# Reading split weights and first operand pairs into the place of their low parts, in a Perceiver block kernel

## The chip, the core and the metric

The kernel runs on one core of a Trainium2 chip. The metric is the device time of one execution in microseconds (us). TensorE (PE) multiplies matrices, VectorE (DVE), ScalarE (ACT) and GpSimd (POOL) work on elements, and SyncE (SP) issues most DMAs. Each engine works through its own instructions in order, and semaphores tie the engines together.

## What is computed

For 2048 tokens (32 sequences of 64) of width 512 the reference adds three residual parts to `x`, each behind a layer norm: a cross attention over a context of 256 rows per sequence, a latent attention with 16 heads, and a feed-forward part. What matters here are the last two:

```python
out = einsum('bshc,hdc->bshd', softmax(scores) @ kv, wkv_b[:, NOPE:])
x = x + out.reshape(bs, seq_len, H * VD) @ wo_w.T + wo_b      # "wo"
h = square(relu(layernorm(x) @ up_w))                         # "up"
y = h @ down_w + (x @ expert_weight) * sum_of_top2(logits)    # "down"
x = x + layernorm(y) * gamma + beta
```

All arithmetic is float32. The kernel gets that precision from fp32r matmuls: every operand is split into a high part (the value rounded to fp32r) and a low part (value minus high part), and a product is three matmuls (high·high, low·high, high·low).

## The kernel before, in words

The program is one function, `perceiver_block`, under a tile framework. The framework lays tiles out in pools of on-chip memory (a pool with `bufs=n` has n rooms that turn), places the semaphore waits, and orders each engine's instructions by the order of the code and by when its own planning takes them to be ready; `with after(x)` (line 135) keeps an instruction behind x on x's engine. The stages, in order:

1. **Cross attention and query/key preparation** (lines 165 to 585).
2. **Latent attention** (lines 587 to 892): 32 units j of (4 head groups g) x (8 token blocks blk). A unit's values are summed on POOL (`b_w`, line 798) and stored to DRAM tiles `v_d` (`store_v`, line 809). In the same loop every big weight is prepared for later: `prep_w` and `prep_sums` (lines 614, 631) write it to a DRAM tile `w_d[what, k]`.
3. **wo** (loop from line 1003): the output projection, as a seven-product scheme of 2x2 blocks. The work is 64 units u = (token block, slot k); k runs over `ORDER = (0, 1, 5, 6, 7, 2, 3, 4)`, and a unit is 21 matmuls (`seven`, line 692) of one operand pair with one weight slot. The first 16 units mix blocks 0 and 1, so that the slots are needed one by one. Layer norm, turned activations and the small expert product of each block are woven in (`o_sum`, `o_norm`, `o_t`, `o_expert`, lines 920 to 998).
4. **up** (from line 1109): 4 token blocks b of 512 x 8 slots n, 42 matmuls each (`up_seven`), followed by a combine on DVE and a squared ReLU on ACT; the results go to DRAM tiles `h_d` (`store_h`, line 1147).
5. **down** (loop from line 1303): again 64 units of `seven`, with pairs read from `h_d`.

Two kinds of operand are read from DRAM and split before PE can use them.

- A **weight slot** is 128 x 7 x 256 float32, 0.918 MB. `read_slot` (line 638) reads it into a room of the pool `cwp` (2 rooms of 8 KB per partition, tiles `cw_...`). `put_slot` (line 643) then fills the slot's own tiles `wh_...` (tag h) and `wl_...` (tag l) by `split` (line 138) in two slices: ACT casts `c` to `h`, DVE computes `l = c - h`. A slot k has one pair of tiles, used in turn by wo, up and down. The pools of slots 0 and 1 exist from the start of latent attention; those of 4, 3, 2, 7, 6, 5 are laid out after it (line 894) over memory that attention's tiles held.
- An **operand pair** (128 x 7 x 128, 0.459 MB) is read by `read_pair` (line 666) into a small room (`c...`, `oc...`) and split by `left` (line 683) into one of three rotating tiles `hl`.

The places that the change touches, as they stand before:

- slots 0 and 1 for wo are read at g = 3, blk = 3 (line 827) and put at blk = 5 and 6; slot `ORDER[2]` is read behind the loop (line 862), `ORDER[3]` at line 880, each later one just ahead of a `put_slot` in the unit loop at `SLOT_AT = (3, 5, 7, 9, 11)`;
- pairs 0 and 1 are read into halves of a `cwp` room (lines 847 to 850);
- the first four up slots are read and put in units 56, 58, 60, 62 of wo (line 1032); four more at the start of up;
- block 7's sums `oo7` use the single room `o` of the pool `ap` (line 917) that block 6's sums leave when their store to `x2_d` has landed;
- in the last block of up (b = 3) slot `ORDER[n+1]` for down is read into `cwp` at step n, and slot `ORDER[n]` is put behind step n, n = 0 to 4; the last three are put in units 1, 3, 5 of down.

Of the kernel before, what the change touches and what calls it, by code (L numbers as in the profile page):

```python
# [9 lines left out]
FP = mybir.dt.float32  # L10
FR = mybir.dt.float32r
# [7 lines left out]
P = 128  # L19
# [32 lines left out]

SLOT_AT = (3, 5, 7, 9, 11)
EXPERT_AT = (15, 16, 17, 18)
TURN_AT = (19, 22, 28, 34, 42, 50, 58)
MULT_AT = (21, 25, 31, 39, 47, 55, 63)

BETA_AT = 60
# [21 lines left out]
def perceiver_block(ctx: ExitStack, tc: tile.TileContext, x, mem, mask, wq_a, bq_a, qnw, wq_b, bq_b,  # L80
# [3 lines left out]
    def pool(name, bufs=1, **kw):  # L84
        return tc.tile_pool(name=name, bufs=bufs, reuse_waits="tile", **kw)
# [92 lines left out]
    with ExitStack() as mla:  # L178
# [409 lines left out]
        with ExitStack() as pb:  # L588
# [4 lines left out]
            one = pb.enter_context(pool("b_one"))  # L593
            sp = pb.enter_context(pool("b_s", 4))
            pp = pb.enter_context(pool("b_p", 2))
            vp = pb.enter_context(pool("b_v", 2))
            qp = pq.enter_context(pool("b_q", 6))
            gap(pq.enter_context(pool("gap10")), 128, "qh1")
            wqs[1] = pq.enter_context(pool("b_w1", 2))
# [34 lines left out]

            def load_slot(k, what):
                put_slot(k, what, read_slot(k, what))

            def read_slot(k, what, cp=None):
                c = (cp or cwp).tile([P, 8, TB], FP, tag="cw", name=f"cw_{what}{k}")[:, 0:7]
                nc.sync.dma_start(c, w_d[what, k])  # L640
                return c

            def put_slot(k, what, c, engine=nc.vector, pins=(None, None)):

                h = slots[k].tile([P, 7, TB], FR, tag="h", name=f"wh_{what}{k}")
                l = slots[k].tile([P, 7, TB], FR, tag="l", name=f"wl_{what}{k}")
                for a in (slice(0, 4), slice(4, 7)):
                    split(h[:, a], l[:, a], c[:, a], engine, pins)
                wts[k] = (h, l)
# [6 lines left out]

            wts = {}

# [7 lines left out]
            def read_pair(u, src, room=None):  # L666
# [14 lines left out]
                cps[u] = c  # L681

            def left(u, room=None, pins=(None, None)):

                hl = room or hlp.tile(0, name=f"hl{u}")
                hl = hl.rearrange("p a n -> p (a n)")
                h, l = (hl[:, 7 * P * i : 7 * P * (i + 1)].rearrange("p (a n) -> p a n", a=7) for i in range(2))
                low = split(h, l, cps.pop(u), pins=pins)
                ops[u] = (h, l)
                return low  # L690
# [123 lines left out]
            gap(ctx.enter_context(pool("gap1", side="right")), 64, "hl")  # L814
            hls = [ctx.enter_context(pool("hl0", side="right"))]
            hlp = Turns(hls)
# [5 lines left out]
            for j in range(n):  # L822
                g, blk = units[j]
                if blk == 0 and g < 3:
                    load_q(2 * g + 2)
                    load_q(2 * g + 3)
                if g == 3 and blk == 3:
                    cs_wo = [read_slot(k, "wo") for k in range(2)]
                t = []

                def between(behind):
                    if j >= 1:
                        b_d(units[j - 1], ss[j - 1], behind)
                    if j >= 2:
                        t.append(b_t(units[j - 2], ss.pop(j - 2)))
                        return copies[-1]

                qs[j], pins = b_q(units[j], between)
                v = b_v(units[j - 2], *t) if j >= 2 else None
                if v and j < n - 1:  # L840
                    v = b_w(*v)
                if g < 3 and 1 <= blk <= 6:
                    split_q(2 * g + 2 + (blk - 1) // NKQ, (blk - 1) % NKQ, pins)
                if g == 3 and blk in (5, 6):
                    put_slot(blk - 5, "wo", cs_wo.pop(0), pins=pins)
                if j == n - 2:
                    pair_room = cwp.tile([P, 8, TB], FP, tag="cw", name="cw_c").rearrange("p a n -> p (a n)")
                    part = lambda i: pair_room[:, 896 * i : 896 * i + 896].rearrange("p (a n) -> p a n", n=P)
                    for u in range(2):
                        read_pair(u, from_v, lambda: part(u))  # L850
                if j == n - 1:
                    left(0, pins=pins)
                ss[j], sub, most = b_s(units[j], qs.pop(j))
                if loaded:
                    with after(sub):
                        prep_sums(*loaded.pop(0))
                if preps:
                    loaded.append(prep_w(*preps.pop(0)))
                if v and j < n - 1:
                    store_v(*v)  # L860

            cs_wo = [read_slot(ORDER[2], "wo")]
            pq.close()
            ps_p = pc.enter_context(pool("o_psp", space=PSUM))
            for i in range(2):
                hls.append(ctx.enter_context(pool(f"hl{i + 1}", side="right")))
            hlp.pools = hls
            gap(ctx.enter_context(pool("gap2", side="right")), 64, "c")
# [9 lines left out]
            left(2)  # L878
            with after(reads[-1]):
                cs_wo.append(read_slot(ORDER[3], "wo"))  # L880
            read_pair(4, from_v)
# [34 lines left out]
    def o_steps(blk, ps):  # L916
        o = ap.tile([P, 5, TB], FP, tag="o", name=f"oo{blk}")
        return o, combine(ap.tile([P, TB], FP, tag="p1", name=f"op1_{blk}"), ps, o, [])
# [81 lines left out]
    mos = {0: ap.tile([P, 2, D], FP, tag="mo", name="mo0")}  # L1000
    put_slot(ORDER[2], "wo", cs_wo.pop(0))
    xt, xns, xT, x2s, read = {}, {}, {}, {}, 5
    for u, (blk, k) in enumerate(out_units):
# [7 lines left out]
        if u >= 2:  # L1011
# [8 lines left out]
            o, steps = o_steps(blk, pss[blk]) if k == ORDER[-1] else (None, None)  # L1020
            seven(pss[blk], k, *ops.pop(u), steps)
        if u in SLOT_AT:
            i = 3 + SLOT_AT.index(u)
            if i < 7:
                with after(reads[-1]):
                    cs_wo.append(read_slot(ORDER[i + 1], "wo"))
            put_slot(ORDER[i], "wo", cs_wo.pop(0), pins=low)
        if u == 10:
            xt[0] = o_load(0)
        if u in EXPERT_AT:  # L1030
            load_expert(EXPERT_AT.index(u))
        if u - 8 * (NB - 1) in (0, 2, 4, 6):
            load_slot(ORDER[(u % 8) // 2], "up")
        if u in TURN_AT:
# [15 lines left out]
        if u in MULT_AT:  # L1050
# [3 lines left out]
            if i < NB - 2:  # L1054
                next(scaled)
    xr, xc = {}, {}

    def read_x(b, kk, room=None):
# [3 lines left out]
        xc[kk] = (t, None if room else t)  # L1062

    def sum_x(b, kk, behind):

        t, w = xc[kk]
        if w is None:
            w = cwp.tile([P, 8, TB], FP, tag="cw", name=f"xc{b}_{kk}")
            xc[kk] = (t, w)
        with after(behind):  # L1070
            sums([t[:, d] for d in range(4)] + [w[:, d] for d in range(4, 8)], RIGHT)

    def right(b, part, pins=(None, None)):
# [8 lines left out]
        with after(pins[low]):  # L1082
            for sl in [slice(1, 8)] if c is w else [slice(1, 4), slice(4, 8)]:
                to, src = slice(sl.start - 1, sl.stop - 1), (c if sl.start == 1 else w)[:, sl]
                if low:
# [6 lines left out]
    for kk in range(2):  # L1092
        read_x(0, kk)
        sum_x(0, kk, pows[-1])
# [10 lines left out]
    with ExitStack() as pu:  # L1105
# [51 lines left out]
        right(0, 3)  # L1157
        up_c = [read_slot(k, "up") for k in ORDER[4:6]]
        for b in range(NB // 2):
            if b == NB // 2 - 1:  # L1160
                first = [(blk, k) for ks in (ORDER[:5], ORDER[5:]) for blk in DOWN[:2] for k in ks]
                out_units[:] = first + [(blk, k) for blk in DOWN[2:] for k in ORDER]
            if b == NB // 2 - 1:
                cs = [read_slot(ORDER[0], "down")]
            for n, k in enumerate(ORDER):
# [4 lines left out]
                if b == 0 and n in (1, 2):  # L1170
                    read_x(1, n - 1, lambda: ccp.tile([P, 8, P], FP, tag="c", name=f"xp{n}").rearrange(
                        "p (a b) n -> p a (b n)", b=2))
                if b == NB // 2 - 1 and n < 6:
                    cs.append(read_slot(ORDER[n + 1], "down"))
                if b == NB // 2 - 1 and n in (5, 6):
# [16 lines left out]
                if b == 0 and n < 4:  # L1192
                    put_slot(ORDER[n + 4], "up", up_c.pop(0), pins=pins)
                    if n < 2:
                        up_c.append(read_slot(ORDER[n + 6], "up"))
                if b == NB // 2 - 1 and n < 5:
                    put_slot(k, "down", cs.pop(0), pins=pins)
                if b == NB // 2 - 1 and n == 2:
# [21 lines left out]
    with ExitStack() as pd:  # L1220
# [82 lines left out]
        for u, (blk, k) in enumerate(out_units):  # L1303
# [19 lines left out]
            if u in (1, 3, 5):  # L1323
                put_slot(ORDER[5 + u // 2], "down", cs.pop(0))
            if u == 1:
                cs.append(read_slot(ORDER[7], "down"))
            outs = [d for d in outs if step(d, low)]
# [52 lines left out]
```

## Time and profile before

| | |
|---|---|
| median of 3 runs | 1113.07 us (1111.52 to 1113.95) |
| the profiled execution's own time | 1114.92 us |
| its span, from first to last instruction | 1113.1 us |
| PE busy | 1069.7 us, 96% of the span |
| DVE, ACT, POOL busy | 772.9, 547.6, 508.0 us |
| DMA | 254.67 MB, mean 229 GB/s |
| wo stage (first `seven` to first `up`) | about 553 to 784 us |
| up stage | 784 to 943 us |
| down stage | 943 to 1113 us |

The profile is one execution seen by the hardware profiler. Times count from the span's start. In a timeline row the columns are start, duration, engine, line of the code, operation, output tile <- input tiles, shape, count, and in brackets the idle time of that engine just before, with what ended it. In a row by stretches the columns are the stretch and its length, the busy time and count of PE, of PE's weight loads, of DVE, ACT and POOL, then the granted PE clock (1.00 is full), the busy share of the DMA engines and GB/s. Lines that are shared helpers (L141 and L143 are the two halves of every split) are told apart by their tiles.

### The profile page before, as it was taken

Reading aid. Unit: us, or ns where it says so; the run is one execution under the profiler, and the core shown is the slowest. Engines: PE = TensorE matmul, PEld = TensorE weight load, DVE = VectorE, ACT = ScalarE, POOL = GpSimd, SP = SyncE. Lnnn points to the kernel's source line nnn. Section 1 sums busy time; section 2 is a strip of 40 time slices with the busy share of each in tenths; the row PEclk is TensorE's granted clock in tenths of the full one; section 3 lists DMA queues with packets and bytes.
Section 4 is the critical chain, followed back from the end, with each engine's and each line's share of the span. In section 5 each row is a group of like instructions: output and inputs, shape, how many; then the busy total and the mean of one; then the engine's idle time right before and its main releaser. Section 6 shows DMA issues by size and latency. Waiting matters only on the chain.

```text
span 1113.1 us, 25983 instructions
## 1 busy us (share of the span) xinstructions
PE 1069.7 (96%) x10182; PEld 984.6 (88%) x10182; DVE 772.9 (69%) x1363; ACT 547.6 (49%) x1048; POOL 508.0 (46%) x694
## 2 busy tenths in 40 slices
PE   8899999999999999999989999998999998999896
PEld 6677777679999999999889999998999998999896
DVE  4666666647666667666878866668776577688796
ACT  4344444433444434433556544445676667564553
POOL 2333333326778777775471100002058770056761
PEclk9999999999999999999999999998999999999999
DMA  8777666343676787772498776776755789998681
GB/s 260 224 229 231 210 213 209 113 159 126 250 243 236 252 285 265 254 250 105 141 363 298 248 240 227 219 265 232 242 189 193 238 291 279 297 314 254 205 246 59
DMA packets 195386, 254.67 MB, mean 229 GB/s; under 512 B 18544, under 2 KB 140032, under 8 KB 195264
## 3 DMA queue, kind: packets, MB, share of 16 engines
q1 hardware_dynamic: 190848, 241.45, 66.1%
q10 hardware_dynamic: 3456, 8.39, 2.1%
q0 software_dynamic: 960, 3.18, 0.9%
q8 instruction: 80, 1.31, 0.5%
q14 instruction: 42, 0.34, 0.1%
HBM read 146.67 MB, written 106.30 MB: 227 GB/s over the span
## 4 chain that ended last, share of the span: by engine, by line
PE 59%; DMA 12%; DVE 11%; POOL 7%; issue 6%; ACT 4%; SPq 1%; DVEq 0%; POOLq 0%; ACTq 0%
PE up L1115 10%; PE pss L749 6%; PE psq L173 4%; PE psq L174 4%; PE psq L175 4%; PE psv L793 3%; PE op L702 2%; PE op L701 2%; PE op L699 2%; PE psc L367 2%; DMA cw_down<-wd_down 2%; DVE hl L143 2%; PE pse L173 2%; PE pse L175 2%; PE pse L174 2%
## 5 line engine op out<-in xcount | busy, mean ns | idle before, releaser
L731 DVE SCALAR_TENSOR_TENSOR qe<-pse,bqp,cq 64x256 f32<-64x256 f32 x256 | 123.8, 483 | 79.4 <-PE pse L175 73.3
L1115 PE MATMUL up<-xr,wh_up 128*128 128x256 f32 x896 | 154.8, 278 | 2.9 <-ACT up L154 2.9
L1115 PEld LDWEIGHTS up<-xr,wh_up 128*128 128x128 f32 x896 | 136.6, 190 | 3.1 <-ACT up L154 3.1
L701 PE MATMUL op<-wh_wo,hl 128*128 128x256 f32 x448 | 125.5, 280 | 4.8 <-DVE hl L143 4.7
L701 PE MATMUL dp<-wh_down,hl 128*128 128x256 f32 x448 | 124.9, 279 | 4.4 <-DVE hl L143 4.4
L143 DVE TENSOR_TENSOR hl<-c,hl 128x896 fp32r<-128x896 f32 x85 | 96.8, 1140 | 45.5 <-ACT hl L141 45.4
L699 PE MATMUL dp<-wh_down,hl 128*128 128x256 f32 x448 | 124.4, 278 | 1.5 <-DVE uo L159 1.5
L699 PE MATMUL op<-wh_wo,hl 128*128 128x256 f32 x448 | 125.5, 280 | 0.3 <-ACT hl L141 0.3
L702 PE MATMUL op<-wl_wo,hl 128*128 128x256 f32 x448 | 124.4, 278 | 0.1
L702 PE MATMUL dp<-wl_down,hl 128*128 128x256 f32 x448 | 124.4, 278 | 0.0
L1115 PE MATMUL up<-xr,wl_up 128*128 128x256 f32 x448 | 122.9, 278 | 0.0
L141 ACT CAST hl<-c 128x896 fp32r<-128x896 f32 x85 | 79.9, 943 | 76.0 <-PE op L702 33.2
L173 PE MATMUL psq<-qa_hi,qh 128*128 128x256 f32 x384 | 112.7, 294 | 0.0
L174 PE MATMUL psq<-qa_hi,ql 128*128 128x256 f32 x384 | 106.6, 278 | 0.0
L175 PE MATMUL psq<-qa_lo,qh 128*128 128x256 f32 x384 | 106.5, 277 | 0.0
L701 PEld LDWEIGHTS op<-wh_wo,hl 128*128 128x128 f32 x448 | 84.4, 188 | 6.5 <-DVE hl L143 6.4
L701 PEld LDWEIGHTS dp<-wh_down,hl 128*128 128x128 f32 x448 | 84.8, 189 | 5.1 <-DVE hl L143 5.0
L699 PEld LDWEIGHTS dp<-wh_down,hl 128*128 128x128 f32 x448 | 84.8, 189 | 1.7 <-issue 1.7
L699 PEld LDWEIGHTS op<-wh_wo,hl 128*128 128x128 f32 x448 | 84.2, 188 | 1.1 <-issue 0.7
L702 PEld LDWEIGHTS dp<-wl_down,hl 128*128 128x128 f32 x448 | 84.8, 189 | 0.0
L1115 PEld LDWEIGHTS up<-xr,wl_up 128*128 128x128 f32 x448 | 84.8, 189 | 0.0
L702 PEld LDWEIGHTS op<-wl_wo,hl 128*128 128x128 f32 x448 | 84.4, 189 | 0.3 <-DVE wl_wo L143 0.3
(227 smaller groups left out, 3152.8 us busy)
## 6 DMA issues: line engine op xcount, KB each, us to landing
c<-vd SPq DMA_DIRECT2D x58, 448.0 KB, 4.3
cx<-in_ctx SPq DMA_DIRECT2D x32, 512.0 KB, 4.6
vd<-vw SPq DMA_DIRECT2D x29, 512.0 KB, 3.8
hd<-uo SPq DMA_DIRECT2D x107, 128.0 KB, 3.4
hd<-uw SPq DMA_DIRECT2D x21, 512.0 KB, 3.0
dcw<-hd SPq DMA_DIRECT2D x18, 448.0 KB, 5.7
vd<-v SPq DMA_DIRECT2D x30, 256.0 KB, 3.3
c<-hd SPq DMA_DIRECT2D x17, 448.0 KB, 5.8
```

The source lines that it names most:

```text
L141: copy = nc.scalar.copy(hi, src)
L143: return copy, engine.tensor_tensor(lo, src, hi.bitcast(FP), ALU.subtract)
L173: nc.tensor.matmul(ps, ah, bh, start=(j == 0), stop=False)
L174: nc.tensor.matmul(ps, al, bh, start=False, stop=False)
L175: nc.tensor.matmul(ps, ah, bl, start=False, stop=(j == n - 1))
L699: first = nc.tensor.matmul(ps[s // 2][:, s % 2], h[:, a], wh[:, b], start=(k == 0 and s % 2 == 0), stop=False)
L701: nc.tensor.matmul(ps[s // 2][:, s % 2], l[:, a], wh[:, b], start=False, stop=False)
L702: ins = nc.tensor.matmul(ps[s // 2][:, s % 2], h[:, a], wl[:, b], start=False, stop=last)
L731: rope = nc.vector.scalar_tensor_tensor(qe[64 * a : 64 * a + 64, :], pe[r, :], bqp[r, p : p + 1], cq[r, a, :], ALU.add, ALU.mult,)
L749: nc.tensor.matmul(ps[64 * j : 64 * j + 64, pj, b, :], qs[2 * pj + j][a][:, sl], kT[:, a, kt], start=(a == 0), stop=(a == 1),)
L793: nc.tensor.matmul(o, kv[a, i, :], t[a, bp, :], start=True, stop=True)
L1115: nc.tensor.matmul(ps[s // 2][:, s % 2], w[:, i, kk], xr[b, 2 * kk + low][:, j], start=(first and m == 0), stop=(last and m == len(parts) ...
```

## The change

- `read_slot` reads a slot straight into its own `l` tile (`home=True`); `put_slot` casts from there to `h` and subtracts in place. `cwp` is then no longer passed through. With `home=False` the slot waits in a `cwp` room as before: this is kept for `ORDER[2]` and `ORDER[3]` of wo, which are now read during attention (g = 3, blk = 4 and 5).
- Pairs 0 and 1 are read into the second half of their `hl` tile (`read_home`); the pool `hl1` is laid out before attention ends. Room for it comes from `b_s` (4 to 2 buffers) and a gap.
- wo slots `ORDER[4..7]` are read at units 1, 2, 4, 6 and put where they were. Up slots `ORDER[0..3]` are read behind units 57, 58, 59, 61 and put behind 58, 60, 61, 63; `ORDER[4]` is read behind 62.
- `oo7` takes a `cwp` room. The rearranged activations of up's first block are read into `c` rooms, with one `cwp` room for their sums; so their split takes two slices instead of one.
- In up's last block slot `ORDER[n-1]` for down is read at step n (n > 0) and slot `ORDER[n-2]` put behind step n (n = 2 to 6); `ORDER[7]` is read in unit 0 of down.

```diff
-SLOT_AT = (3, 5, 7, 9, 11)
+READ_AT, SLOT_AT = (1, 2, 4, 6), (3, 5, 7, 9, 11)
+UP_READ, UP_PUT = (1, 2, 3, 5, 6), (2, 4, 5, 7)
-            sp = pb.enter_context(pool("b_s", 4))
+            sp = pb.enter_context(pool("b_s", 2))
...
+            def room_of(k, what):
+                return [slots[k].tile([P, 7, TB], FR, tag=a, name=f"w{a}_{what}{k}") for a in ("h", "l")]
+            def read_slot(k, what, home=True, behind=None):
+                hl = room_of(k, what) if home else None
+                c = hl[1].bitcast(FP) if home else cwp.tile([P, 8, TB], FP, tag="cw", name=f"cw_{what}{k}")[:, 0:7]
+                with after(behind):
+                    read_slots[what, k] = hl, c, nc.sync.dma_start(c, w_d[what, k])
+            def put_slot(k, what, pins=(None, None)):
+                hl, c, _ = read_slots.pop((what, k))
+                h, l = hl or room_of(k, what)
                 for a in (slice(0, 4), slice(4, 7)):
-                    split(h[:, a], l[:, a], c[:, a], engine, pins)
+                    split(h[:, a], l[:, a], c[:, a], pins=pins)
...
+            def read_home(u, src):
+                blk, k = out_units[u]
+                homes[u] = hlp.tile(0, name=f"hl{u}")
+                cps[u] = homes[u].rearrange("p a n -> p (a n)")[:, 7 * P :].rearrange("p (a n) -> p a n", a=7).bitcast(FP)
+                reads.append(nc.sync.dma_start(cps[u], src(blk, k)))
...
                 if g == 3 and blk == 3:
-                    cs_wo = [read_slot(k, "wo") for k in range(2)]
+                    for k in range(2):
+                        read_slot(k, "wo")
+                if g == 3 and blk in (4, 5):
+                    read_slot(ORDER[blk - 2], "wo", False)
...
-        o = ap.tile([P, 5, TB], FP, tag="o", name=f"oo{blk}")
+        if blk < NB - 1:
+            o = ap.tile([P, 5, TB], FP, tag="o", name=f"oo{blk}")
+        else:
+            o = cwp.tile([P, 8, TB], FP, tag="cw", name=f"oo{blk}")[:, 0:5]
...
+        if u in READ_AT:
+            read_slot(ORDER[4 + READ_AT.index(u)], "wo", behind=reads[-1])
         if u in SLOT_AT:
-            i = 3 + SLOT_AT.index(u)
-            if i < 7:
-                with after(reads[-1]):
-                    cs_wo.append(read_slot(ORDER[i + 1], "wo"))
-            put_slot(ORDER[i], "wo", cs_wo.pop(0), pins=low)
+            put_slot(ORDER[3 + SLOT_AT.index(u)], "wo", pins=low)
-        if u - 8 * (NB - 1) in (0, 2, 4, 6):
-            load_slot(ORDER[(u % 8) // 2], "up")
+        if u - 8 * (NB - 1) in UP_READ:
+            read_slot(ORDER[UP_READ.index(u % 8)], "up")
+        if u - 8 * (NB - 1) in UP_PUT:
+            put_slot(ORDER[UP_PUT.index(u % 8)], "up", pins=low)
...
-                if b == NB // 2 - 1 and n < 6:
-                    cs.append(read_slot(ORDER[n + 1], "down"))
+                if b == 0 and n in (0, 1):
+                    read_slot(ORDER[n + 6], "up")
+                if b == NB // 2 - 1 and n > 0:
+                    read_slot(ORDER[n - 1], "down")
...
-                if b == NB // 2 - 1 and n < 5:
-                    put_slot(k, "down", cs.pop(0), pins=pins)
+                if b == NB // 2 - 1 and 1 < n < 7:
+                    put_slot(ORDER[n - 2], "down", pins=pins)
...
             if u in (1, 3, 5):
-                put_slot(ORDER[5 + u // 2], "down", cs.pop(0))
-            if u == 1:
-                cs.append(read_slot(ORDER[7], "down"))
+                put_slot(ORDER[5 + u // 2], "down")
+            if u == 0:
+                read_slot(ORDER[7], "down")
```

## Prediction

> **What bounds the kernel now.** I began with the busy times: TensorE (PE) works 1069.7 us of the 1113.1 us span, VectorE (DVE) 772.9, and the count of matmuls is not touched by the change. So the change can only win PE's idle time, and what its clock loses behind idle time. The view of waits for PE says where that idle time lies; these are its rows in the stages that the change touches:
>
> ```profile
> PE op L701 <- DVE hl L143: 4.7, 6, 1.3
> ...
> PE ops L959 <- DVE on L133: 3.2, 1, 3.2
> PE up L1115 <- ACT up L154: 2.9, 1, 2.9
> ...
> PE dp L699 <- DVE uo L159: 1.5, 1, 1.5
> ```
>
> Some 12 us in 9 waits, three places: the start of wo (L701), the end of wo (L959, block 7's norm before its activations are turned), and the step from up to down (L1115 and L699). The timeline gives when and behind what. First PE's five longest of these waits, then the ScalarE (ACT) casts ahead of them:
>
> ```profile
> 582.35 0.39 PE L701 MATMUL op<-wh_wo,hl 128*128 128x256 f32 x1 [1.10 <-DVE hl L143]
> 589.32 0.38 PE L701 MATMUL op<-wh_wo,hl 128*128 128x256 f32 x1 [1.23 <-DVE hl L143]
> 774.46 0.45 PE L959 MATMUL ops<-ident,on 128*128 128x128 f32 x1 [3.19 <-DVE on L133]
> 925.85 0.35 PE L1115 MATMUL up<-xr,wh_up 128*128 128x256 f32 x1 [2.91 <-ACT up L154]
> 943.53 0.36 PE L699 MATMUL dp<-wh_down,hl 128*128 128x256 f32 x1 [1.49 <-DVE uo L159]
> ```
>
> ```profile
> 578.11 1.79 ACT L141 CAST wh_wo<-cw_wo 128x1024 fp32r<-128x1024 f32 x2 [4.01 <-DMA cw_wo<-wd_wo]
> 585.02 1.79 ACT L141 CAST wh_wo<-cw_wo 128x1024 fp32r<-128x1024 f32 x2 [3.44 <-DMA cw_wo<-wd_wo]
> 921.87 1.05 ACT L141 CAST wh_down<-cw_down 128x1024 fp32r<-128x1024 f32 x1 [3.45 <-DMA cw_down<-wd_down]
> ```
>
> The reader is to see that ACT, an engine 49% busy, stood 3.4 to 4.0 us for a weight slot to land, with the next pair's cast or the block's copy out of PSUM queued behind it. PE got those too late. Last, the stretches, with the granted clock, DMA share and GB/s in the last three columns:
>
> ```profile
> 580.00:588.00 8.00, 6.64 (x53) 6.13 (x52) 5.13 (x6) 4.56 (x6) 0.00 (x0) 1.00 1.02 420
> 758.00:770.00 12.00, 11.67 (x98) 11.38 (x97) 9.53 (x14) 4.42 (x6) 0.00 (x0) 1.00 0.95 338
> 774.40:784.20 9.80, 9.74 (x57) 9.19 (x58) 6.01 (x9) 6.75 (x9) 5.81 (x7) 0.69 0.51 178
> 904.00:924.00 20.00, 18.94 (x164) 18.74 (x162) 14.26 (x21) 12.07 (x21) 11.43 (x12) 1.00 1.06 343
> 925.90:931.00 5.10, 5.10 (x31) 5.10 (x32) 4.57 (x8) 4.57 (x8) 0.00 (x0) 0.67 0.90 252
> 956.00:1016.00 60.00, 59.27 (x518) 58.78 (x517) 47.83 (x60) 33.90 (x54) 19.79 (x26) 1.00 1.05 302
> ```
>
> Two things. The DMA engines are full at the start of wo and from 904 to 1016: there a transfer that is only moved gains nothing. And the clock fell behind the two longest waits: 0.69 over 9.8 us is 9.8 x 0.31 = 3.0 us lost after 774.4, and 0.67 over 5.1 us is 1.7 us after 925.9. Waits of 1.1 to 1.5 us were not followed by a lower clock. The Trainium skill, "TensorE: Matmul & The Clock Gate", section "Why this matters for your kernels", asks for no PE gap over about 3 us; here 2.91 us already brought it down, so row and rule differ a little, and by the rule alone the 925.85 wait would have cost 1.7 us less.
>
> **Start of wo.** A unit of wo is 21 matmuls, 2.38 us. Measured by the starts of the matmuls, the stalls from 570 to 598 sum to 5.75 us (1.49, 0.76, 1.27, 0.43, 1.50, 0.30). The first two (2.25) lie under back-to-back DVE work from 566 to 577, which the change leaves: they stay. The other 3.5 come from casts behind slots that landed late (issued 569.53, landed 578.09; 574.63 to 585.00; 581.32 to 589.87). *Removed*: `ORDER[2]` and `ORDER[3]` are read during attention, so one slot of 0.918 MB leaves a stretch that moves 354 GB/s from 554 to 592, that is 2.6 us of the DMA engines; the others start 4 to 10 us sooner. *Added*: nothing on the engines, since the cast and the subtract keep their sizes (a slot 1.06 + 0.83 us on ACT, 2.09 on DVE). In place, the subtract has a row elsewhere: `ql<-ql,qh` takes 559 ns where the same shape from another tile takes 557, so I put it at 0. *A new wait*: `ORDER[6]`'s low part lies, by the layout of the pools, over rooms that attention's last values leave only when their stores land: issued by GpSimd (POOL) at 577.41, landed 585.83. The read stands in SyncE's (SP) queue at unit 4, some 571, and pairs 10 to 13 and slot `ORDER[7]` stand behind it. With the stretch a slot lighter I put the last store at about 582. Pair 10 was issued at 577.72 and is used at unit 10, about 585; a landing took 8.6 to 10 us there. So 0 to 1.3 us come back. Bounds: -3.5 (all gone) to +2.5 (rival B). I take 3.5 - 1.3 = **-2.2**, nearest to the rows of the waits.
>
> **End of wo.** Block 7's sums no longer wait for block 6's store (issued 760.97, landed 766.79): DVE's row is `oo<-op,op` at 766.91, 0.76 us idle before it on DMA. That 0.77 goes in whole, as it stands in the chain to 774.46. The late units had stalls of some 1.1 us by the starts (752, 757, 763), of which I count half: ACT's cast of an up slot at 762.97 stood 2.56 us for its DMA. Against: the first up slots were read at 717 to 725 and can now be read only when wo's last matmul with that slot is over, from 746; so five slots, 4.6 MB, crowd into 746 to 770, where 263 to 338 GB/s were already moved. And the last put is behind unit 63: 2.1 us of DVE that may now stand before the norm (+2). Best case: the 3.19 us wait shrinks to under 1.5 and the clock loss of 3.0 goes as well: -5.3 with the combine earlier. I take 0.77 + 0.5 and a third chance of the clock, 0.9: **-2.2**. The split of up's first activations in two slices costs 0.82 + 1.05 instead of 1.70 us on ACT and 0.95 + 1.22 instead of 2.02 on DVE, from the rows of later blocks: +0.15 each, under the 1.84 us of POOL sums at 771 to 774.5; without that cover +0.2.
>
> **Up to down.** Now the read stands ahead of its put by two steps of 4.77 us, and a landing there took 4.4 to 8.5 us (median 6.2): ACT doesn't stand, the copy at 925.44 comes in time. The wait of 2.91 goes, its clock loss of 1.7 too, and of the 1.49 at 943.53 perhaps half: -5.3. Against: `ORDER[0]`'s slot, read at 887.20 before, is now read at about 903, when its up matmuls are done: 0.918 MB more in the full stretch from 904, 2.7 us at 343 GB/s. The only slack is 924 to 944 with 0.85 (252 against 350 GB/s: 2 MB). And slots put at n = 5 and 6 bring DVE 2.09 + 2.6 (combine) + 1.09 (pair) = 5.8 us in a step of 4.77. What comes late then is pairs 6, 10 and 16 to 20 of down, used 0 to 2 us after their splits. I give back 2.8: **-2.5**, between -6 and +2. The Trainium skill, "DMA: Bandwidth & Descriptors", section "Rules for kernel authors", says to issue a DMA early and wait late; it speaks against this part, since reads into the slot's own tile must start later (887.2 to about 903; 717 to 746). By it alone my estimate would be a loss of one landing, up to 8 us, at the end of wo or in down.
>
> **The sum**: -2.2 - 2.2 - 2.5 = -6.9. Against the profiled execution, 1114.92 us (span 1113.1 and 1.8 outside it), 1108.0; that execution lies 1.85 above the median of 1113.07, so the forecast is **1106.2**. A measurement here can tell about 0.2%, 2.2 us, from no change.
>
> **Rivals.**
>
> *A, the DMA engines take it back.* What the slots win is paid by the pairs, since no byte less is moved: two slots fall into full stretches (2.6 + 2.7 us), the clock falls as before. Left is 2.2 of wo's start: 1113.07 - 2.2 = 1110.9, about 1111. For it: 1.02 to 1.06 in the DMA column. Against: 924 to 944 has room, and ACT's waits are for order, not bytes.
>
> *B, slower: SP stands behind `ORDER[6]`.* If POOL's last stores land as before, at 585.8, the read, and pairs 10 to 13 behind it in SP's queue, are issued 8 us later than pair 10 was (577.72). Pair 10 lands then at about 592, and with its split of 2 us PE needs it at 585: a stall of 4 to 7 us, over the 2.91 that halved the clock, so 1.7 more, less the 3.5 that goes: +2.5 to +5, and with the late reads giving nothing at the other places 1113.07 + 3.5 = 1116.5. It decides as soon as that store lands after about 583. Against: the DMA stretch is a slot lighter, and the stores were issued by 577.4.
>
> *C, all three places clear*, both clock losses gone: -3.5 - 5.3 - 6.0 = -14.8, 1098.3. For it: each wait named is one that the change removes. Against: the full DMA engines.
>
> *That it does nothing* would show as the same casts standing for DMA; that is in A.
>
> **Chances.** Forecast 0.44 (1101 to 1110), A 0.19, B 0.21, C 0.16. Faster by over 0.2% (below 1110.8): 0.44 + 0.16 + 0.02 of A = 0.62; within: 0.15 of A + 0.01 of B = 0.16; slower: 0.20 of B + 0.02 of A = 0.22. The range, 1097 to 1117, leaves out the low half of C and the upper part of B. For the likeliest case alone it is 1101 to 1110.
>
> **What would show it.** Right: no cast of `wh_wo` or `wh_down` standing for DMA at 578 to 590 and 922; the wait before L959's first matmul below 3 us; no stretch of half clock at 927. B: SP's read of `ORDER[6]` issued behind POOL's landing, and units 10 to 13 starting late. A: DMA at 1.0 from 904 with new PE waits in down. The forecast falls if slots read at 746 to 765 hold the last units of wo, or if the put behind unit 63 stands before the norm and keeps the 3.19 us.

## The result and the profile after

The changed kernel is slower: 1120.68 us median of 7 runs (1117.34 to 1127.82) against 1113.86 for the kernel before (7 runs, 1111.52 to 1115.07), a ratio of 1.0070 with a 95% interval of 1.0047 to 1.0092. The forecast was 1106.2, the range 1097 to 1117. The profiled execution took 1117.83 us (span 1116.1), one of the quicker ones; a second one, taken later, took 1125.35 (span 1123.6).

The waits of TensorE (PE) after the change, in us in total, times, longest. Line numbers have moved: L710 to L713 are `seven`, L969 the turns of a block, L1132 the up matmuls, L175 a shared triple of matmuls, L143 and L145 the two halves of a split.

```profile
PE op L710 <- ACT hl L143: 4.1, 1, 4.1
PE dp L712 <- DVE hl L145: 3.6, 4, 1.6
...
PE op L712 <- DVE hl L145: 3.6, 3, 2.5
PE pse L175 <- ACT qn L738: 3.0, 3, 2.3
...
PE ops L969 <- DVE on L135: 2.9, 1, 2.9
```

Of the places in the prediction the step from up to down (2.91 and 1.49 before) is gone from the list; a wait of 1.6 on a pair's split (L712) is new there. Block 7's turns (L969) wait 2.91 instead of 3.19. The start of wo has a wait of 4.15 where the longest was 1.32 (at 570.56). And attention (`pse`) has one that was not there. The timeline shows what stands behind the two new ones (start, duration, engine, line, operation, and in brackets the idle time just before on that engine or queue):

```profile
281.33 0.94 ACT L143 CAST hl<-hl 128x896 fp32r<-128x896 f32 x1 [6.91 <-DMA hl<-vd]
...
283.58 0.39 PE L175 MATMUL pse<-qa_hi,qh 128*128 128x256 f32 x1 [2.33 <-ACT qn L738]
...
569.09 1.19 SPq L684 DMA_DIRECT2D c<-vd  x2
585.54 0.32 SPq L645 DMA_DIRECT2D wl_wo<-wd_wo  x1
...
581.93 0.72 POOL L823 DMA_DIRECT2D vd<-vw  x1
...
592.22 0.38 PE L710 MATMUL op<-wh_wo,hl 128*128 128x256 f32 x1 [4.15 <-ACT hl L143]
```

**At 283 us**, a quarter into the kernel, ScalarE (ACT) stands 6.91 us for the transfer of an operand pair that wo needs at 558, and attention's query copies wait behind its cast. (Before the change this pair was read at 538 and cast at 551; now it is read at 273.) **At 592 us** it is rival B: SyncE's queue (SPq) issues nothing from 570.3 to 585.54. Its next entry is the read of slot `ORDER[6]`, which waits for POOL's last store of values, issued at 581.93; by the trace that store landed at 585.34, 0.2 us earlier. Pairs 10 to 14 and slot `ORDER[7]` stood behind that read.

To see what each stretch gained or lost, I compared the times between the same matmuls in both traces. The differences (of the unrounded times) sum to 2.6 us; the spans differ by 2.9, and the rest lies almost all ahead of the first stretch. A second pair of profiles, further down, shows how much of each line belongs to the execution.

| stretch, first profiles | before | after | difference |
|---|---|---|---|
| latent attention | 313.2 | 316.3 | +3.1 |
| start of wo (units 0 to 10) | 36.9 | 39.1 | +2.2 |
| the 43 us behind it | 42.1 | 43.3 | +1.2 |
| middle of wo | 125.9 | 126.1 | +0.1 |
| end of wo, block 7's turns | 24.5 | 22.5 | -2.0 |
| up | 122.4 | 127.0 | +4.6 |
| step from up to down | 47.8 | 43.8 | -3.9 |
| down | 145.4 | 142.7 | -2.6 |

The +4.6 in up has no wait in it at all. The rows by stretches (last columns: PE clock, DMA share, GB/s) show it; first the kernel before, then the changed one:

```profile
800.00:850.00 50.00, 50.00 (x444) 50.00 (x443) 35.71 (x61) 34.54 (x61) 29.36 (x39) 1.00 0.63 201
```

```profile
593.00:597.00 4.00, 3.66 (x19) 3.66 (x20) 3.69 (x5) 2.96 (x4) 0.00 (x0) 0.57 1.01 408
800.00:850.00 50.00, 50.00 (x427) 50.00 (x426) 33.73 (x59) 35.13 (x61) 17.23 (x24) 1.00 0.50 155
```

In 50 us of dense PE work at full granted clock there are 444 matmuls before and 427 after: 113.3 ns from start to start against 117.8. The row 593:597 shows the second price of the long wait: half clock for one window of 3.41 us.

### The profile page after: what moved, and what is told of

It reads as the page before. It is cut to its first block, busy times and chain, and to the rows that moved or that the text cites. A ratio compares the mean times of both kernels' runs of the same rounds, so it can differ in the third digit from the quotient of the medians.

```text
span 1116.1 us, 26007 instructions
## 1 busy us (share of the span) xinstructions
PE 1074.0 (96%) x10182; PEld 990.3 (89%) x10182; DVE 771.5 (69%) x1365; ACT 546.1 (49%) x1050; POOL 505.5 (45%) x694
## 4 chain that ended last, share of the span: by engine, by line
PE 65%; DVE 10%; DMA 9%; POOL 7%; issue 5%; ACT 4%; SPq 0%; DVEq 0%; POOLq 0%; ACTq 0%
PE up L1132 14%; PE pss L760 5%; PE psq L175 4%; PE psq L176 3%; PE psq L177 3%; PE op L712 3%; PE op L710 3%; PE op L713 3%; PE psv L804 3%; DMA c<-vd 2%; PE psc L369 2%; DVE hl L145 2%; PE pse L175 2%; PE pse L177 2%; PE pse L176 2%
## 5 line engine op out<-in xcount | busy, mean ns | idle before, releaser
L1132 PE MATMUL up<-xr,wh_up 128*128 128x256 f32 x896 | 158.3, 281 | 0.0
L1132 PEld LDWEIGHTS up<-xr,wh_up 128*128 128x128 f32 x896 | 136.9, 188 | 0.0
L710 PE MATMUL op<-wh_wo,hl 128*128 128x256 f32 x448 | 125.5, 282 | 4.1 <-ACT hl L143 4.1
L712 PE MATMUL op<-wh_wo,hl 128*128 128x256 f32 x448 | 125.4, 281 | 3.6 <-DVE hl L145 3.6
L145 DVE TENSOR_TENSOR hl<-c,hl 128x896 fp32r<-128x896 f32 x85 | 98.4, 1161 | 43.6 <-ACT hl L143 43.4
L712 PE MATMUL dp<-wh_down,hl 128*128 128x256 f32 x448 | 124.6, 278 | 3.6 <-DVE hl L145 3.6
L713 PE MATMUL op<-wl_wo,hl 128*128 128x256 f32 x448 | 124.7, 280 | 0.0
L1132 PE MATMUL up<-xr,wl_up 128*128 128x256 f32 x448 | 124.3, 281 | 0.0
L713 PE MATMUL dp<-wl_down,hl 128*128 128x256 f32 x448 | 124.1, 277 | 0.0
L710 PE MATMUL dp<-wh_down,hl 128*128 128x256 f32 x448 | 123.8, 277 | 0.0
L143 ACT CAST hl<-c 128x896 fp32r<-128x896 f32 x85 | 79.9, 941 | 79.4 <-PE op L713 37.1
L175 PE MATMUL psq<-qa_hi,qh 128*128 128x256 f32 x384 | 112.9, 294 | 0.0
L712 PEld LDWEIGHTS op<-wh_wo,hl 128*128 128x128 f32 x448 | 85.1, 190 | 4.6 <-DVE hl L145 4.4
L710 PEld LDWEIGHTS op<-wh_wo,hl 128*128 128x128 f32 x448 | 84.5, 189 | 5.2 <-ACT hl L143 4.3
L712 PEld LDWEIGHTS dp<-wh_down,hl 128*128 128x128 f32 x448 | 84.1, 188 | 4.4 <-DVE hl L145 4.4
L1132 PEld LDWEIGHTS up<-xr,wl_up 128*128 128x128 f32 x448 | 85.7, 191 | 0.0
L713 PEld LDWEIGHTS op<-wl_wo,hl 128*128 128x128 f32 x448 | 84.9, 190 | 0.0
L710 PEld LDWEIGHTS dp<-wh_down,hl 128*128 128x128 f32 x448 | 84.4, 189 | 0.0
L713 PEld LDWEIGHTS dp<-wl_down,hl 128*128 128x128 f32 x448 | 84.1, 188 | 0.0
```

What stands on the lines that cost most here:

```text
L143: copy = nc.scalar.copy(hi, src)
L145: return copy, engine.tensor_tensor(lo, src, hi.bitcast(FP), ALU.subtract)
L175: nc.tensor.matmul(ps, ah, bh, start=(j == 0), stop=False)
L710: first = nc.tensor.matmul(ps[s // 2][:, s % 2], h[:, a], wh[:, b], start=(k == 0 and s % 2 == 0), stop=False)
L712: nc.tensor.matmul(ps[s // 2][:, s % 2], l[:, a], wh[:, b], start=False, stop=False)
L713: ins = nc.tensor.matmul(ps[s // 2][:, s % 2], h[:, a], wl[:, b], start=False, stop=last)
```

## The experiments

All are timed beside the kernel before on their own chip, in five rounds; the last two are one execution each. "Faster by 2 us" and the like compare ratios to that kernel times 1112.5. In nearly all of them executions spread over 6 to 13 us, the kernel before too (1107.91 to 1118.09 in 29 runs).

**Pin one cast** (`e1_pin`). Pair 1's cast had no pin on ACT; pair 0's had.

```diff
-            left(1, pins=(None, most))
+            left(1, pins=(pins[0], most))
```

> The changed kernel, but the cast of pair 1 into its high part is kept behind the last query copies of the loop, as pair 0's is. Main theory (the loss is made of waits that the new rooms let in): the cast no longer stands at 281 us in ScalarE's queue for its transfer, so the 2.33 us wait of TensorE at 283.6 goes: 1118.2 us (1117 to 1119.5) against 1120.7 for the change as it is. Rival (the loss is one of full DMA engines and of the slower matmul rhythm, 117.8 instead of 113.3 ns, in up): no wait of this size counts, 1120 to 1121, and the wait turns up at the start of wo.

1119.45 us, ratio 1.0066 (1.0040 to 1.0092): hardly less than 1.0070. The wait at 283 is gone and attention is back to 313.5 us, but the other wait grew. SyncE's queue stops sooner, and stands longer, ahead of the read of `ORDER[6]`:

```profile
563.81 1.22 SPq L684 DMA_DIRECT2D c<-vd  x2
582.03 0.32 SPq L645 DMA_DIRECT2D wl_wo<-wd_wo  x1
...
588.76 0.47 PE L710 MATMUL op<-wh_wo,hl 128*128 128x256 f32 x1 [5.03 <-ACT hl L143]
```

The stage wo began 4 us earlier (554.0), POOL's last store landed 3.5 us earlier (581.83), and half clock behind the wait lasted two windows (6.83 us) instead of one. So the gain is taken away at the next bound. The time lies at the upper end of the main theory's range and its interval reaches into the rival's; the profile shows the wait of the main theory gone and the wait at the start of wo of the rival, with the queue and not the rhythm of up behind it. The landing at 581.83 matters for the account of the prediction below.

**Let the slot that is needed last lie over the late rooms** (`e2_late7`).

```diff
-    for k in (4, 3, 2, 7, 6, 5):
+    for k in (3, 4, 2, 7, 6, 5):
-READ_AT, SLOT_AT = (1, 2, 4, 6), (3, 5, 7, 9, 11)
+READ_AT, SLOT_AT = (1, 2, 4, 8), (3, 5, 7, 9, 11)
```

> The changed kernel, but the pools of slots 3 and 4 change places, so that the last slot of ORDER and not the last but one lies over the rooms of attention's last values, and that slot is read at unit 8 instead of 6. Main theory (rival B of the forecast): SyncE's queue no longer stands with pairs 10 to 13 behind it; the waits of 4.15 + 0.74 us at 592 and the half clock behind them (1.7) go: 1114 us (1112 to 1117). Rival (the DMA engines are full at the start of wo, so the transfers land late in any order): a wait of over 3 us stays in units 10 to 15, 1119 to 1121.

1114.16 us, 1.0011 (0.9992 to 1.0030): 6.6 us less than the changed kernel, as expected. The last slot's read still waits for the store, with one pair behind it instead of five. Here and in `e1_pin` and `e3_both` too the read is issued 0.2 us behind that store's landing (590.04 to 590.21 here). PE's longest wait at the start of wo is 1.1 us and the stretch takes 33.0 us, 4.0 less than before the change; 1.7 of these come back in the 43 us behind it (43.8).

**Both** (`e3_both`).

> Both edits of e1_pin and e2_late7. Main theory: the two gains add up, 2.5 + 6.6 us, to 1111.5 us (1109 to 1114.5), faster than the kernel before. Rival (full DMA engines): 1118 to 1121. If up runs at 117.8 ns a matmul in the profile, 6 us of it is that rhythm.

1109.78 us, 0.9978 (0.9960 to 0.9996). With the second wait away the pin is worth 3.7 us (1.0011 to 0.9978) where alone it was worth 0.4; the two intervals just overlap, but attention agrees (316.2 us in `e2_late7`'s profile, 312.9 here). The start of wo takes 32.5 us (36.9 before), the stretch behind it 43.9 (42.1). What is left of the waits, and what stands ahead of them:

```profile
PE dp L712 <- DVE hl L145: 3.4, 2, 2.1
...
PE ops L969 <- DVE on L135: 2.9, 1, 2.9
...
PE dp L710 <- ACT hl L143: 1.5, 1, 1.5
```

```profile
758.40 3.22 DVE L145 TENSOR_TENSOR wl_up<-wl_up,wh_up 128x1024 fp32r<-128x1024 f32 x3
761.54 0.68 DVE L158 TENSOR_TENSOR oo<-op,op 128x512 f32<-128x512 f32 x1
...
935.53 1.78 ACT L143 CAST wh_down<-wl_down 128x1024 fp32r<-128x1024 f32 x2 [3.78 <-DMA wl_down<-wd_down]
```

Block 7's sums (`oo<-op`) have their room, but the subtractions of two up slots are ahead of them on VectorE (DVE). And in up's last block ACT again stands for a slot.

**The down part alone, on the kernel before** (`e4_down`): a slot is read into its own tile at step n for `ORDER[n-1]`, put behind step n for `ORDER[n-2]`.

```diff
-                if b == NB // 2 - 1 and n < 6:
-                    cs.append(read_slot(ORDER[n + 1], "down"))
+                if b == NB // 2 - 1 and n > 0:
+                    cs.append(read_slot(ORDER[n - 1], "down", home=True))
...
-                if b == NB // 2 - 1 and n < 5:
-                    put_slot(k, "down", cs.pop(0), pins=pins)
+                if b == NB // 2 - 1 and 1 < n < 7:
+                    put_slot(ORDER[n - 2], "down", cs.pop(0), pins=pins)
```

> The kernel before, with only the last part of the change: in up's last block the slots for down are read into their own low parts one step after their matmuls and put one step later. Main theory: the step from up to down wins what it won in the changed kernel, 5.9 us by the starts of the matmuls, and 2.1 come back at the start of down: 1110 us (1108 to 1112) against 1113.9. Rival (the stretch from 904 to 1016 is full, so what is read later is paid later): 1113 to 1115.

1111.31 us, 0.9992 (0.9973 to 1.0010): no difference that shows. The profile has the old wait of 2.91 away, new ones of 2.21 and 2.08 at 944 to 947 with a window of half clock, and the step at 48.6 us (47.8 before). The 5.9 us that I read off the changed kernel (the table's stretch has 3.9) were not the edit's alone: its up ran at the slower rhythm, where a step of 42 matmuls leaves the other engines 0.2 us more by my estimate, and its second profile below, at the quicker rhythm, takes 49.8 us for the step.

**The opposite: `e3_both` without the down part** (`e8_nodown`), slots through the waiting rooms as before.

> e3_both without the down part of the change: the slots for down go through the waiting rooms again, a step ahead of their matmuls, as in the kernel before. If that part is worth the forecast's 2.5 us: 1112.3 us (1111 to 1114). If it is worth nothing as it stands, as e4_down's 0.9 (from -3 to +1) and the profile's step of 48.1 us against 47.8 before let me think: 1109 to 1111, with the kernel before's wait of 2.9 us at the copy of up's sums back.

1112.09 us, 0.9995 (0.9977 to 1.0012) against 0.9978 with the part. The two intervals overlap; the ratios differ by 1.9 us. The old wait of 2.9 us, which one half of the expectation had coming back, is not in its profile, where up ran at 117.8 ns.

**Puts one step later in that part** (`e6_dlate`, on `e3_both`).

```diff
-                if b == NB // 2 - 1 and 1 < n < 7:
-                    put_slot(ORDER[n - 2], "down", pins=pins)
+                if b == NB // 2 - 1 and n > 2:
+                    put_slot(ORDER[n - 3], "down", pins=pins)
```

> e3_both, but in up's last block slots for down are put one step later (ORDER[n-3] behind steps n = 3 to 7). Main theory (ScalarE stood 3.78 us for a slot's transfer at 935.5 in e3_both with the squared ReLUs queued behind it, and TensorE's waits of 1.47 and 2.08 us at 942 to 945 come from that): those waits fall below 1 us together and the half clock at 943 goes, 4 us less: 1106 us (1104 to 1108). Rival (the stretch is bound by the DMA engines and VectorE, so the order of the puts is of no use): the same waits come back in the first units of down, 1109 to 1111.

1107.48 us, 0.9952 (0.9933 to 0.9972). In its profile one wait of 0.74 us is left in the step from up to down, and no half clock:

```profile
935.00:960.00 25.00, 23.81 (x202) 23.05 (x201) 22.22 (x27) 19.84 (x27) 0.00 (x0) 1.00 1.05 315
```

The DMA engines are as full as ever (1.05), so full engines alone do not make these waits. Against `e8_nodown` (0.9977 to 1.0012) the intervals are apart: in this form the down part is worth 4.8 us. Against `e3_both` (0.9960 to 0.9996) they overlap. And this profile ran up at 117.8 ns. The three later kernels with the same puts (`e7_all`, `e9_end2`, `e12_oo7`) ended up at 113.3 ns, and each has a wait of 1.6 to 1.7 us at 944 to 948, a second of 0.74 or 0.75, and one window of half clock, where `e3_both` had 1.47 and 2.08 us and two windows. So the later put shortens the waits; the profile above shows them shorter than these three do.

**Up's last two slots behind block 7's norm** (`e5_end`, on `e3_both`; `e7_all` has the edits of `e5_end` and `e6_dlate`).

```diff
-UP_READ, UP_PUT = (1, 2, 3, 5, 6), (2, 4, 5, 7)
+UP_READ, UP_PUT = (1, 2, 3, 5, 6), (2, 4)
...
         right(0, part, xT[2])
+    for k in ORDER[2:4]:
+        put_slot(k, "up", pins=(low[0], xT[2][1]))
```

> e3_both, and the last two of the four up slots that wo's last units put (slots ORDER[2] and ORDER[3]) are subtracted on VectorE behind block 7's norm and its turned activations, not ahead of the sums. Main theory (the later puts stand before the norm and keep the wait that the free room for block 7's sums should end): the 2.90 us wait before block 7's turns falls below 0.8, the two windows of half clock at 769 go with it (3.4 us), so 4 to 5 us less than e3_both: 1105.5 us (1103.5 to 1107.5) where the kernel before takes 1112.4. Rival (it only moves work: the low parts of up's first activations are late instead): 1109 to 1111, with a new wait at the start of up.

> Both edits of e5_end and e6_dlate. Main theory: 8 us less than e3_both, 1102 us (1099 to 1105). Rivals of both: 1108 to 1111.

1111.98 us, 0.9995 (0.9976 to 1.0014), and for both edits 1111.20, 0.9991 (0.9967 to 1.0014): no gain, so here the rival was right. The wait at the turns fell from 2.90 to 0.88, and up began with a new one, since the subtractions now stood between the low parts of up's first activations:

```profile
785.33 0.58 PE L1134 MATMUL up<-xr,wh_up 128*128 128x256 f32 x1 [3.44 <-ACT mo L1005]
```

**The same, pinned behind those low parts** (`e9_end2`, on `e6_dlate`).

```diff
-        right(0, 3)
+        last = right(0, 3)
+        for k in ORDER[2:4]:
+            put_slot(k, "up", pins=(low[0], last))
```

> e6_dlate, and the subtractions of up slots ORDER[2] and ORDER[3] on VectorE kept behind the last low part of up's first activations (in e5_end they stood between those parts and the wait only moved, from 2.9 us at block 7's turns to 3.44 at the start of up). Main theory: neither wait is left, 2.9 us and the half clock behind it (1.7 to 3.4) less than e6_dlate's 1107.5: 1103.5 us (1101.5 to 1105.5) where the kernel before takes 1113. Rival (VectorE is simply full from wo's last unit to up's second step, and what is put off is late for steps 2 and 3 of up): 1106.5 to 1109, with a wait at those steps.

1107.03 us, 0.9951 (0.9932 to 0.9971). Neither wait is left; the end of wo takes 19.8 us (23.0 in `e6_dlate`'s profile, 24.5 in the first of the kernel before), with full clock:

```profile
761.00:770.00 9.00, 8.90 (x75) 8.70 (x75) 6.46 (x16) 4.10 (x8) 0.62 (x1) 1.00 1.01 350
770.00:782.00 12.00, 10.66 (x86) 10.03 (x85) 10.59 (x14) 7.87 (x13) 8.04 (x10) 1.00 0.97 373
```

But the time is that of `e6_dlate`, 0.9952. 3.3 us are within what two such intervals allow (each 2 us wide on either side). The profile also has waits that `e6_dlate`'s does not have, the rival's in up and one in down with half clock behind it:

```profile
794.80 0.36 PE L1132 MATMUL up<-xr,wh_up 128*128 128x256 f32 x1 [0.93 <-DVE uo L161]
947.42 0.39 PE L710 MATMUL dp<-wh_down,hl 128*128 128x256 f32 x1 [1.63 <-ACT hl L143]
```

So part of the gain was lost again in this execution; how much of it in all executions is open. Both kernels beat the kernel before and the changed one.

**Block 7's sums in their old room** (`e12_oo7`, on `e9_end2`).

> e9_end2 with block 7's sums in the single room of the activations' pool again, as in the kernel before, so that they wait for block 6's store. In e9_end2's profile that store landed at 763.48 us and the sums began at 763.63, released by TensorE. Theory: the free room is worth nothing by itself once the store is issued at that time: 1107 us (1105.5 to 1109), the wait before block 7's turns stays below 1.5. Rival (the 0.77 us of the forecast, and the half clock that a longer wait brings): 1109 to 1111, with VectorE waiting for the store and over 2 us before the turns.

1110.10 us, 0.9978 (0.9962 to 0.9994). Its profile says "worth little": the sums waited for the store (landed 760.35), and PE's wait at the turns was 0.92 us against 0.88. Its time says 3 us. The profiled execution took less than `e9_end2`'s, and the intervals overlap. PE waited 3.0 us in three waits for sums in up (L1129 are its up matmuls), where `e9_end2` has one of 0.93; whether the room has to do with that was not tested. Unclear.

**Both kernels once more with a profile** (`e10_before`, `e11_after`, nothing changed).

> The kernel before, once more with a profile, and nothing changed. Theory (TensorE has two rhythms in dense stages, 113.3 and 117.8 ns a matmul, and falls into either by chance of the execution): some of its stages run at the other rhythm than in the first profile, where up and down ran at 113.3. Rival (the rhythm belongs to the kernel, by its tiles' places and order): every stage as in the first profile.

> The changed kernel, once more with a profile, and nothing changed. First profile: up at 117.8 ns a matmul, the first part of down at 113.3, its end at 117.8. Theory (by chance of the execution): up or down at another rhythm. Rival (by the kernel): the same. Either way the waits at 283 (2.3 us) and 592 (4 us or more, and half clock behind) are there again, since they come from the order of the queues.

The same stage, first the kernel before, then the changed kernel (its up stage lies 20 us later):

```profile
800.00:850.00 50.00, 50.00 (x427) 50.00 (x426) 35.16 (x61) 33.48 (x59) 30.73 (x41) 1.00 0.62 195
```

```profile
825.00:875.00 50.00, 50.00 (x444) 50.00 (x443) 33.38 (x59) 34.10 (x60) 34.57 (x44) 1.00 0.58 188
```

The kernels have changed sides: 427 matmuls before, 444 after. So the rhythm isn't the kernel's, and the +4.6 us of up in the first pair of profiles is no part of the loss. The second execution of the changed kernel took long all the same, 1125.35 us, and its waits say why:

```profile
PE op L712 <- DVE hl L145: 5.1, 4, 3.3
PE op L710 <- ACT hl L143: 4.9, 1, 4.9
PE pse L175 <- ACT qn L738: 4.3, 3, 3.6
```

The two waits are back and longer, with half clock behind each. The step from up to down, which looked won in the first profile, has two waits and two windows of half clock:

```profile
961.02 0.74 PE L710 MATMUL dp<-wh_down,hl 128*128 128x256 f32 x4 [2.00 <-ACT hl L143]
963.84 0.58 PE L712 MATMUL dp<-wh_down,hl 128*128 128x256 f32 x1 [2.08 <-DVE hl L145]
```

And the kernel before's wait of 2.91 us at that step, with 1.7 us of half clock behind it, is shorter in its second execution, without half clock:

```profile
925.88 0.35 PE L1115 MATMUL up<-xr,wh_up 128*128 128x256 f32 x1 [1.30 <-ACT up L154]
```

| stretch | before, first | before, second | after, first | after, second |
|---|---|---|---|---|
| latent attention | 313.2 | 313.4 | 316.3 | 322.5 |
| start of wo | 36.9 | 35.1 | 39.1 | 40.5 |
| end of wo | 24.5 | 23.1 | 22.5 | 23.3 |
| up | 122.4 | 127.0 | 127.0 | 122.8 |
| step from up to down | 47.8 | 46.0 | 43.8 | 49.8 |
| down | 145.4 | 143.7 | 142.7 | 140.2 |

Of these lines only the losses in attention and at the start of wo, and some gain in down, stand in both pairs.

**The clock of all executions** sums this up. One minus the granted clock, times the span, is at most the time taken by half clock (where PE idles it costs nothing, and some 4 us of it lie behind the last matmul): 14.6 us on average over the changed kernel's 7 runs, 14.7 in `e1_pin`, 9.5 in `e2_late7`, 9.0 in `e3_both`, 7.5 over 29 runs of the kernel before. By this sum up to 7.1 us of the changed kernel's loss (6.8 us by the medians, 8.0 by the means) are half clock. Of them `e2_late7`, without the wait at 592, has 5.1 back; `e1_pin`, without the wait at 283, none. Single profiles vary: the first pair has 12.1 us before and 9.9 after, the second 9.9 and 18.0.

## Why the prediction was wrong, point by point

With the two waits repaired (`e3_both`) the change wins 2.4 us (0.4 to 4.4 by the interval), not 6.9: the forecast lacked one term, had the price of another wrong, and counted as gains at two places what was in part one execution's.

- **Start of wo (-2.2 forecast, +2.2 and +5.4 in the two pairs of profiles).** The step that failed is "So 0 to 1.3 us come back", the price of the queue behind the read of `ORDER[6]`. It was 4.15 + 0.74 us and a window of half clock, and 6.6 us by the time of `e2_late7`; rival B had 4 to 7 and 1.7. "I put the last store at about 582" failed too: it landed at 585.34, beyond the 583 from which I let rival B decide, as attention ended 3 us later and POOL issued the store at 581.93 instead of 577.41. But that did not decide it. In `e1_pin` wo begins at 554.0 (554.9 before the change) and the store lands at 581.83, as I had put it, and PE waits 5.03 us. SyncE's queue came to that read at 565, not at 571, and stood 17 us. My own rows spoke against the small price: behind a store at 582, a landing of 8.6 to 10 us and a split of 2 us bring pair 10 at 592.6 or later, and unit 10 wants it at about 585.
- **The gain there.** It exists: units 3 to 15 take 34.6 us in `e3_both` and 37.5 and 37.4 in the profiles of the kernel before. But it does not lie where I put it. The first two stalls (2.25 us), which I let stay, are gone (units 3 to 8 take 14.6 us after the change, 18.2 and 17.0 before), while waits of up to 1.3 us stand behind unit 8 in `e3_both`. So that 2.9 is near my 3.5 is luck. My list of PE's longest waits also left out the longest at this place, 1.32 us at 570.56.
- **Attention (0 forecast, +3.1 in the first profiles, +9.1 in the second).** Not in my sum at all: the prediction does not speak of reading the first pairs into their own tiles. In the old room in `cwp` pair 1 was read at 538.07 and its unpinned cast came at 551; in its own tile it is read at 272.96 and the cast stands at 281, among attention's. `e1_pin` shows that the missing pin is the cause of the wait. That the old room's later release had kept the read and the cast in their place I take from the code; it was not tested by itself. A room taken away is also a wait taken away, and I did not ask what the wait had been holding.
- **End of wo (-2.2 forecast, -2.0 in the first pair of profiles, +0.1 in the second).** The sums no longer waited for the store, as forecast. My own objection, that the last put may stand before the norm, came true: 2.90 to 2.91 us stay at the turns, with half clock, until `e5_end` and `e9_end2` move two slots. That the first pair agrees with the forecast is luck: 1.7 of its 2.0 us are one window of half clock instead of two, and the kernel before's second profile has one as well.
- **Up to down (-2.5 forecast).** In the changed kernel's form it is worth about 1.9 us (`e3_both` against `e8_nodown`) and by itself 0.9 (`e4_down`), neither clear of nothing. "ACT doesn't stand" failed: in `e3_both` a landing took 8.57 us at 927 to 935.5, just above the 4.4 to 8.5 that I quoted, and ACT stood 3.78 us. The 2.91 + 1.7 us that I wanted to win were one execution's: the second has 1.30 and no half clock. With one step more the part is worth 4.8. The rule of the Trainium skill that I had weighed against this part ("DMA: Bandwidth & Descriptors", section "Rules for kernel authors") asks for an early issue and a late wait; `e6_dlate` (0.9952 against 0.9995 without the part) agrees with the late wait, and the later issue alone (`e4_down`, 0.9992) cost nothing that shows.
- **The clock.** I let 2.91 us be the mark. `e3_both` lost two windows behind 1.47 and 2.08 us that lay 0.7 us apart, so waits close together count together (the last section has the sum that the traces show). The Trainium skill's bound of some 3 us for one gap ("TensorE: Matmul & The Clock Gate", section "Why this matters for your kernels") is too wide for that case by these rows. Over the executions the wait at 592 cost up to 5.1 us by the clock besides its own 4.15 + 0.74. The two sum to more than the 6.6 us that `e2_late7` gained, so not all of them was time lost; but the 1.7 that I foretold for the clock was low for an average execution.

## What to carry to other kernels

When a buffer becomes free earlier, look for the instructions that its wait had held in place, and pin them: an unpinned instruction at the head of an in-order engine is a stall for all behind it. Before laying a transfer's target over rooms that are left late, ask what stands behind that transfer in its queue, and give the latest room to what is needed last. And with several waits in a row, removing the first alone may show nothing; judge it with the next one away. A wait or a window of half clock read off one profile may be that execution's: a second profile of the same kernel tells.

## What the runs showed of the hardware

- In dense stretches at full granted clock PE ran in one of two rhythms, 113.3 or 117.8 ns from matmul to matmul (128x256, each with its own weight load), and stayed in it until some small gap. In the kernel before's first profile one matmul came 166 ns instead of 113 behind the last, at 913 us, and all after it followed at 117.8 until the next long wait. Up alone takes 122.4 or 127.0 us by it. The changed kernel's two executions and the kernel before's two had one of each. It does not explain their times: in each kernel the execution with the slower up was the quicker one (1112.89 against 1114.92 us, 1117.83 against 1125.35). What sets the rhythm wasn't found, and the granted clock does not show it.
- The half-clock windows inside a trace all start on one grid of 3.41 us and, but for the one at the program's end, last one or two of its steps. I summed PE's idle time (the ends of matmuls are modelled) in every step of that grid in all 14 traces (from 5 us on, without the last steps). All 37 steps with over 1.9 us idle were followed by half clock; of the 4377 at full clock with under 1.4 us none was, and of the 24 between 6 were. So what counts is the idle time within a step, from one wait or several: 2.06 us of the 2.91 ahead of 925.85 lay in one step, and of the two waits in `e3_both` 1.82 and 1.73 us in two steps.
- The same in-place subtraction of a slot took 3.17 us at 579, while POOL summed values, and 2.08 us at 584, when POOL was idle (in the changed kernel's first profile). The Trainium skill, "SBUF — State Buffer", section "Who interferes with whom", names VectorE's two-input operations and GpSimd's reads as contenders; these rows agree.
